# Router weights by a DRAM broadcast, and the values of four batches together with q and k, in a four-block transformer on one core

## The chip, the core and the metric

The kernel runs on one core of a Trainium2 chip. The metric is device time in microseconds for one execution, as the median of several runs. TensorE is the matmul engine, VectorE, ScalarE and GpSimd are the three engines for elementwise work, and SyncE issues most of the DMAs. Every engine works through its own queue in order.

## The reference

Input x has 32 batches of 128 tokens and 144 channels. Four blocks follow one another; each is steered by a condition vector per batch.

```python
x = _L0_cond_ref(x, ...)   # attention with normalised q, k; MLP
x = _L1_cond_ref(x, ...)   # rotation by expm of a skew matrix, per batch
x = _L2_cond_ref(x, ...)   # attention, MLP
x = _L3_cond_ref(x, ...)   # attention, mixture of experts
```

What matters here is the attention of L2 and L3, and the router and the experts of L3:

```python
h = _modulate(_ln(x), sh_msa, sc_msa)
qkv = (h @ w_qkv + b_qkv).reshape(B, N, 3, nh, hd).transpose(2, 0, 3, 1, 4)
q, k, v = (qkv[0], qkv[1], qkv[2])
attn = softmax(einsum('bhqd,bhkd->bhqk', q, k) * hd ** (-0.5))
...
xn = _modulate(_ln(x), sh_mlp, sc_mlp)
gate_logits = xf @ w_gate                      # 4 experts
topk_logits, topk_idx = top_k(gate_logits, 2)
gates = softmax(topk_logits)
cw = sum(one_hot(topk_idx, 4) * gates[..., None], axis=1)
hmid = gelu(einsum('tc,ech->eth', xf, w1) + b1)
eo = einsum('eth,ehc->etc', hmid, w2) + b2
moe = einsum('te,etc->tc', cw, eo)
```

## The kernel before

All of x stays in SBUF as `x_sb` (128 tokens by 32 batches by 144). The batches go in groups of four (`G`). The 144 channels are split into a main part of 128 rows and a remainder of 16. `ln_T` (L678) normalises, transposes and modulates a group: `hM` holds the main parts; the remainders of the four batches come into one tile `hG` of 128 rows (32 for each batch), which a round trip through DRAM (`hD`) spreads into `hR`, where each of four groups of 32 rows holds the remainders of all four batches. So a product with 144 channels is a main matmul of 128 rows and a remainder matmul of 32 rows on one of four row tiles of the array. `both` (L715) issues the mains of several products and then the remainders, or the other way round, and yields between the two.

PSUM has eight banks: one is `ps_o`, the other seven rotate in order of allocation (`bank`, L82).

The order of the work is written out by hand. The main loop (L1435) runs over ticks, one batch of attention in each. Within a tick it calls `scores` (L880) for half the heads, `weigh` (L939, probabilities by values), `scores` for the other half, and the closing steps (`largest_T`, `largest`, `project_out`, `project_sum`), and between these named gaps ("a", "e", "t", "stats", "b0", "b", "den", "pre1", "c", "y1", "y2", "y3", "z", "d") that `fill` (L1422) fills with whatever `put(tick, gap, f, ...)` has put there. `put2` puts the two halves of a function that yields once in two gaps. The block L0 is layer 0, L2 is layer 1 and L3 is layer 2 in these names; L1, the rotation, is done between them. A group of layer n starts at tick `t0`; its MLP or experts run at `t0 + 7` and later, beside the attention of later groups and layers.

Around the change:

- `qk_chunks` (L752), in gap "c" of `t0 - 2`, makes q and k of a group: three banks of 128x512, three mains, three remainders on row tiles 0 to 2. ScalarE copies them to `qT` and `kT`, and SyncE moves nine rows of each of four heads within SBUF.
- `values` (L851) makes the values of two batches at a time, as tokens by channels, in layers 1 and 2 at `t0` and `t0 + 1`: two banks, two mains (`ps_v`, L720), two remainders on two row tiles, and then four VectorE copies (L863, L864) straight from PSUM into `vaug`.
- `gate_logits` (L1096), at `t0 + 7` in gaps "den" and "c": four mains and four remainders (L1102), the latter with `hR`. `expert_ranks` and `expert_weights` (L1110, L1133) make `cw` at `t0 + 8`, with the last product at L1139.
- `moe1` makes the hidden layer of a pair of experts in three parts; the two experts share one tile of it, `hid[:, SHARED]`, 64 rows each. `shared_by_gate` (L1166) multiplies that tile by the router's weights: GpSimd spreads `cw` to `cwx` (L1171) in "stats", four transposes (L1175) bring it to a bank in "y1", and VectorE multiplies (L1176). This is done for both pairs of a group, at `t0 + 8` and `t0 + 10`.
- `moe2_parts` (L1182) follows in "y2" and "y3": eight records of `ps_f` with the unshared tiles (L1187), then the shared tile (L1192), then two VectorE sums into `acc` (L1196, L1198). In layer 2 the first pair of a group's values stands between the two halves, in "y2".
- `moe_out` (L1200), at `t0 + 12` in gap "b", which is `t0 + 8` of the next group: GpSimd multiplies `acc` by a gate and adds it to x (L1205, L1206), and SyncE writes the group out (L1207).

Matrix products in fp32 stand in the profile as two records each, transposes as one.

Of the kernel before, what the change touches and what calls it, by code (L numbers as in the profile page):

```python
# [8 lines left out]
F32 = mybir.dt.float32  # L9
# [3 lines left out]
ALU = mybir.AluOpType  # L13
# [56 lines left out]
def tile_kernel(ctx: ExitStack, tc: tile.TileContext, a: dict, out: bass.AP):  # L70
# [181 lines left out]
        nms.append(t)  # L252

    take_nm = ring([128, 128], "nm", 2, fill_nm)
    take_kT = ring([128, 4, G * T], "kT", 2, lambda t: None)
    take_qk = ring([128, 32, SLOT], "qkn", 2, fill_qk)
    take_v = ring([128, 2 * NH, 32], "vaug", 2, fill_v)
# [86 lines left out]
    def prep_qr():  # L344


        ala = pq.tile([128, D], F32, name="ala")
        tri = cst[:, K_TRI : K_TRI + D]
        for j in range(D):
            n = C - j  # L350
            cols = slice(j, C + j + 1)
            ps = bank([128, C + 1], f"ps_qr{j}")
            nc.tensor.matmul(
                ps, ident[:, j : j + 1].to_broadcast([128, 128]), at[:, cols], start=True, stop=True
            )
# [38 lines left out]
        nc.vector.tensor_scalar(sgn, sgn, 2.0, -1.0, ALU.mult, ALU.add)  # L394
        nc.vector.tensor_tensor(v[:, :D], v[:, :D], dg, ALU.add)
        yield
        yield
        ps = bank([D, D], "ps_yr")
        nc.tensor.matmul(ps, ident[D:, D:], at[D:, :D], start=True, stop=True)
        y = pq.tile([D, D], F32, name="y")  # L400
        nc.scalar.copy(y, ps)
        yield
        ps = bank([128, C + 1], "ps_uT")
        for h in range(2):
            rows = slice(h * D, (h + 1) * D)
# [12 lines left out]
        nc.gpsimd.memset(uR, 0.0)  # L418
        yield
        yield  # L420
        ps = bank([128, 2, D], "ps_u")
        nc.tensor.transpose(ps[:, 0, :], uT[:D, :CM], idd)
        nc.tensor.transpose(ps[:, 1, :], ur, idd)
        nc.vector.tensor_copy(uM, ps[:, 0, :])
        for i in range(G):
            nc.vector.tensor_copy(uR[rows4(i), i, :], ps[rows4(i), 1, :])

    def prep_expm():

# [322 lines left out]
    def qk_chunks(g):  # L752
# [7 lines left out]
        yield from both(  # L760
            [(ps, p.wqk[:, c], hM) for ps, c in zip(pss, cols)],
            [(ps, p.wqkR[rows4(m), cols[m]], hR[rows4(m)]) for m, ps in enumerate(pss)],
            False,
        )
# [11 lines left out]
        for j in range(4):  # L776
            r = 32 * j + 1
            nc.sync.dma_start(
                kT[r : r + HD, 3, :], qT[r + PITCH : r + PITCH + HD, 1, :]
            )  # L780

    def qk_masked(g):
        kT, k = gr[g].pop("k")
# [311 lines left out]

    def gate_logits(g):  # L1096
        gr[g]["lg"] = lg = small.tile([128, G, E], F32, tag="lg", name=f"lg_{g[1]}", bufs=2)
        hM, hR = gr[g]["hM_m"], gr[g]["hR_m"]
        ps = bank([128, T], f"ps_g_{g[1]}")
        for w, h in ((L3.wgate, hM), (L3.wgateR, hR)):  # L1100
            for i in range(G):
                nc.tensor.matmul(ps[rows4(i)], w, h[:, i, :], start=h is hM, stop=h is hR)  # L1102
        lgT = late.tile([128, T], F32, tag="lgT", name=f"lgT_{g[1]}")
        nc.scalar.copy(lgT, ps)
        yield
# [4 lines left out]
    def expert_ranks(g):  # L1110
# [2 lines left out]
        lg = gr[g]["lg"]  # L1113
        sh = [128, G, E]
        sh4 = [128, G, E, E]
        cw = small.tile(sh, F32, tag="cw", name=f"cw_{g[1]}", bufs=2)
        rank = small.tile(sh, F32, tag="rank", name=f"rank_{g[1]}", bufs=2)
        one = small.tile([128, G, 1], F32, tag="one", name=f"one_{g[1]}", bufs=2)
        gt = small.tile(sh4, F32, tag="gt", name=f"gt_{g[1]}", bufs=2)
# [46 lines left out]
    def shared_by_gate(g, pair):  # L1166


        cwx = late.tile([128, G, 2, 64], F32, tag="cwx", name=f"cwx_{g[1]}_{pair}", bufs=1)
        cw = gr[g]["cw"][:, :, 2 * pair : 2 * pair + 2]  # L1170
        nc.gpsimd.tensor_copy(cwx, cw.unsqueeze(3).to_broadcast([128, G, 2, 64]))  # L1171
        yield
        ps = bank([128, G, T], f"ps_cw_{g[1]}_{pair}")
        for i in range(G):
            nc.tensor.transpose(ps[:, i, :], cwx[:, i, :, :].rearrange("p e c -> p (e c)"), ident)  # L1175
        nc.vector.tensor_tensor(hid[:, SHARED], hid[:, SHARED], ps, ALU.mult)  # L1176

    def moe2(g, e, i):
        for _ in moe2_parts(g, e, i):
# [142 lines left out]
    for layer in range(3):  # L1322
        ahead = 5 if layer == 0 else 6
        for n in range(NG):
# [34 lines left out]
            if layer == 0:  # L1359
                for i in (0, 2):  # L1360
                    put2(t0 + i // 2, "stats", "b", values, g, i, 2, True)
            elif layer == 1:
                put2(t0, "stats", "b", values, g, 0, 2, True)
                put2(t0 + 1, "stats", "b", values, g, 2, 2, True)
            else:
                put2(t0, "y2", "y2", values, g, 0, 2, True)
                put2(t0 + 1, "den", "pre1", values, g, 2, 2)
            if layer:
                put2(t0 - 2, "c", "c", qk_chunks, g)
                if g == (1, 0):  # L1370
# [15 lines left out]
                for i in range(G):  # L1386
                    put(t0 + (10, 10, 11, 11)[i], "bdbc"[i], mlp2, g, i)
            else:
                put2(t0 + 7, "den", "c", gate_logits, g)
                put(t0 + 8, "e", expert_ranks, g)  # L1390
                put(t0 + 8, "stats", expert_weights, g)
                for i in range(G):
                    put(t0 + 8 + i // 2, "cdab"[i], moe_bias, g, i, n == NG - 1)
                for pair in range(2):
# [4 lines left out]
                    else:  # L1399
                        put2(at_, "den", "pre1", moe1, g, pair, 1, False)  # L1400
                    put2(at_ + 1, "stats", "b0", moe1, g, pair, 2, True)
                    put2(at_, "stats", "y1", shared_by_gate, g, pair)
                    put2(at_, "y2", "y3", moe2_parts, g, 2 * pair, 0)
                    put(at_ + 1, "b", moe2, g, 2 * pair, 1)
                    put(at_ + 1, "c", moe2, g, 2 * pair, 2)
# [10 lines left out]
    put(-4, "z", without_means)  # L1416

    put(first[1] - 2, "a", lambda: [zeros(t) for t in nms])
    put(first[1] + B - 10, "c", load_L3)
    put(first[1] + B + 7, "d", lambda: load_pair(1, mlps[:, :PAIR_COLS]))  # L1420

    def fill(tick, gap):  # L1422
# [12 lines left out]
    for tick in range(-6, first[2] + B + 14):  # L1435
# [13 lines left out]
        fill(tick, "stats")  # L1449
        if s2 is not None:  # L1450
            weigh(s2)
        fill(tick, "b0")
        fill(tick, "b")
        fill(tick, "den")
# [209 lines left out]
```

## Time and profile before

| | |
|---|---|
| median of 3 runs | 1283.43 us (1283.4 to 1290.53) |
| profiled execution | 1298.18 us, span 1296.5 us |
| mean granted TensorE clock | 0.988 |
| `ps_cw` L1175, 64 transposes | 10.4 us busy |
| `ps_v` L720, layers 0 and 1: 128 main and 128 remainder records | 23.6 and 14.8 us busy |
| `ps_v` L720, layer 2: 64 main and 64 remainder records | 11.5 and 8.2 us busy |
| `ps_qk` L720, remainders, 96 records | 18.2 us busy |
| VectorE L1176, 16 products of 128x512 | 10.9 us busy, 682 ns each |
| VectorE L863 and L864, 128 copies of 128x72 | 28.5 us busy |
| TensorE waiting for `hR_m` at L1102 | 4.4 us in 2 places, the longest 4.0 |

Busy times are unions of the records of one kind, so 64 overlapping transposes of 285 ns each come to 10.4 us. In a timeline, what an operation costs TensorE is the distance from its start to the start of what follows. Bracketed times are the engine's idle time before a record, with what released it. SyncE's rows show the issue of a DMA, not its transfer.

### The profile page before, as it was taken

The page shows a single profiled execution, that of the slowest core. Times are in us where ns is not written, and L with a number is a line of the kernel's source. Part 1 is how long each engine was busy: PE and PEld are TensorE (multiplying, and loading weights), DVE is VectorE, ACT ScalarE, POOL GpSimd, SP SyncE. Part 2 cuts the span into 40 slices and gives each one's busy share as a digit, 9 for nine tenths or more (in the row PEclk, how much of TensorE's full clock was granted, in tenths as well). Part 3 has the DMA queues.
Part 4 walks back from the last instruction along what each step waited for, and adds up shares of the span by engine and source line. Part 5 has one row for each costly group of instructions (what it writes and reads, how often), then busy time and mean ns, then how long its engine had stood idle before and what let it go on. Part 6 is the DMA issues. An engine that isn't in the chain of part 4 may idle for free.

```text
span 1296.5 us, 35389 instructions
## 1 busy us (share of the span) xinstructions
PE 1243.1 (96%) x13980; PEld 909.2 (70%) x13980; DVE 809.9 (62%) x2543; ACT 779.3 (60%) x1724; POOL 668.4 (52%) x1642
## 2 busy tenths in 40 slices
PE   6889888999998999999999999999999999999998
PEld 5668667778766677677777766667676767677656
DVE  5488888876775467676667666446454646455343
ACT  2457677688685656667666666555555555555431
POOL 5467767756663545454545454636363636251610
PEclk9989999999998999999999999999999999999999
DMA  8200011010013111111121111210101010100000
GB/s 223 65 14 23 16 36 37 2 37 11 30 36 112 62 47 35 46 55 37 47 85 55 55 38 54 76 54 10 55 10 54 11 54 11 54 20 17 20 26 10
DMA packets 50328, 56.44 MB, mean 44 GB/s; under 512 B 4688, under 2 KB 35792, under 8 KB 49904
## 3 DMA queue, kind: packets, MB, share of 16 engines
q1 hardware_dynamic: 49504, 53.70, 13.7%
q8 instruction: 113, 1.85, 0.6%
q10 hardware_dynamic: 656, 0.44, 0.2%
q14 instruction: 55, 0.45, 0.1%
HBM read 39.94 MB, written 13.00 MB: 41 GB/s over the span
## 4 chain that ended last, share of the span: by engine, by line
PE 67%; DVE 3%; DMA 2%; ACT 1%; SPq 1%; issue 0%; POOL 0%; DVEq 0%
PE ps_h L720 19%; PE ps_f L1187 10%; PE ps_s L917 6%; PE ps_w L917 6%; PE ps_o L948 5%; PE ps_qk L720 5%; PE ps_f L1042 4%; PE ps_pj L1012 3%; PE ps_v L720 2%; PE ps_f L1192 1%; DVE nm L929 1%; PE ps_o L869 1%; DMA hD_m<-hG_m 1%; DMA hR_m<-hD_m 1%; PE ps_hT_m L689 1%; PE ps_cw L1175 1%
## 5 line engine op out<-in xcount | busy, mean ns | idle before, releaser
L929 DVE TENSOR_REDUCE nm<-ps_s 128x4 f32<-128x512 f32 x384 | 246.4, 683 | 101.8 <-PE ps_w L917 80.5
L933 ACT ACTIVATE pr<-ps_w 128x512 f32<-128x512 f32 x384 | 208.5, 595 | 150.0 <-PE ps_w L917 141.2
L917 PE MATMUL ps_s<-kT,qT 32*128 32x256 f32 (+2 forms) x1536 | 238.3, 413 | 0.9 <-ACT kT L849 0.9
L917 PE MATMUL ps_w<-q,kT 32*128 32x128 f32 x3072 | 233.7, 287 | 0.0
L917 PEld LDWEIGHTS ps_w<-q,kT 32*128 32x128 f32 x3072 | 197.7, 190 | 11.2 <-issue 6.3
L1036 ACT ACTIVATE hid<-ps_h 128x512 f32<-128x512 f32 (+1 forms) x224 | 119.9, 590 | 101.8 <-PE ps_h L720 101.4
L917 PEld LDWEIGHTS ps_s<-kT,qT 32*128 32x128 f32 x1536 | 138.3, 188 | 30.2 <-issue 10.0
L720 PE MATMUL ps_h<-hM_m,mlps 128*128 128x512 f32 x304 | 144.1, 607 | 0.0
L1196 DVE SCALAR_TENSOR_TENSOR acc<-ps_f,cw,acc 128x144 f32<-128x144 f32 x128 | 46.7, 366 | 148.0 <-PE ps_f L1187 72.9
L998 POOL TENSOR_TENSOR x_sb<-x_sb,res_a 128x144 f32<-128x144 f32 x96 | 46.9, 489 | 158.8 <-DVE res_a L1001 158.0
L948 PE MATMUL ps_o<-pr,vaug 128*32 128x128 f32 x3072 | 105.8, 279 | 0.0
L948 PEld LDWEIGHTS ps_o<-pr,vaug 128*32 128x32 f32 x3072 | 79.4, 111 | 33.7 <-PE ps_w L917 17.4
L720 PEld LDWEIGHTS ps_h<-hM_m,mlps 128*128 128x128 f32 x304 | 53.3, 189 | 67.6 <-issue 66.5
L1042 PE MATMUL ps_f<-mlps,hid 128*128 128x144 f32 x640 | 94.7, 296 | 0.0
L1042 PEld LDWEIGHTS ps_f<-mlps,hid 128*128 128x128 f32 x640 | 83.4, 192 | 8.9 <-issue 4.6
L933 ACT ACT_TABLE_LOAD x57 | 73.1, 1283 | 10.0 <-PE ps_w L917 9.1
L792 POOL TENSOR_SCALAR kT<-kT,cst 128x512 f32<-128x512 f32 x30 | 46.8, 1561 | 58.5 <-ACT kT L774 57.0
L1033 ACT ACT_TABLE_LOAD x58 | 74.4, 1283 | 1.0
L660 POOL TENSOR_SCALAR rs_m_a<-mv_m_a 128x2 f32<-128x2 f32 x81 | 15.5, 191 | 114.3 <-DVE mv_m_a L658 86.5
L1187 PEld LDWEIGHTS ps_f<-pair,hid 128*128 128x128 f32 x512 | 66.9, 190 | 8.4 <-issue 7.7
L1187 PEld LDWEIGHTS ps_f<-mlps,hid 128*128 128x128 f32 x512 | 66.7, 190 | 8.1 <-issue 7.4
L1187 PE MATMUL ps_f<-mlps,hid 128*128 128x144 f32 x512 | 71.3, 288 | 0.0
(337 smaller groups left out, 2747.0 us busy)
## 6 DMA issues: line engine op xcount, KB each, us to landing
gates<-gates SPq DMA_DIRECT2D x48, 288.0 KB
hD_m<-hG_m SPq DMA_DIRECT2D x24, 256.0 KB
hR_m<-hD_m SPq DMA_DIRECT2D x24, 256.0 KB
hD_a<-hG_a SPq DMA_DIRECT2D x16, 256.0 KB
hR_a<-hD_a SPq DMA_DIRECT2D x16, 256.0 KB
x_sb<-in_x SPq DMA_DIRECT2D x8, 288.0 KB
out_x<-x_sb SPq DMA_DIRECT2D x7, 288.0 KB
mlps<-in_L_mlp SPq DMA_DIRECT2D x2, 1000.0 KB
```

Of the source, the lines that this page charges most:

```text
L720: nc.tensor.matmul(ps, x, y, start=k == 0, stop=k == 1)
L792: eng.tensor_scalar(o, k, m, None, ALU.mult)
L917: nc.tensor.matmul(o, x, y, start=True, stop=True)
L929: nc.vector.tensor_reduce(to, view, AX.X, ALU.max, negate=True)
L933: nc.scalar.activation(pr[:, 4 * e : 4 * e + 4, :].rearrange("p s q -> p (s q)"), view, AF.Exp, scale=SCALE,)
L948: nc.tensor.matmul(po[rows4(j), t, :], v[:, 4 * j + 2 * t + r, :], prs[j // 2][:, 4 * (j % 2) + 2 * r + t, :], start=r == 0, stop=r == 1,)
L998: nc.gpsimd.tensor_tensor(x_sb[:, b, :], x_sb[:, b, :], t, ALU.add)
L1033: nc.scalar.activation(t, half, AF.Gelu_apprx_tanh)
L1036: nc.scalar.activation(hid[:n, i], ps[:n], AF.Gelu_apprx_tanh)
L1042: nc.tensor.matmul(ps, hid[:, at0, i, :], w2[:, m, :], start=m == 0, stop=m == NFC - 1)
L1187: nc.tensor.matmul(ps[:, 0, :], hid[:, at0 + m, i, :], w2[:, at0 + m, :], start=m == 0, stop=m == 3)
L1196: nc.vector.scalar_tensor_tensor(acc, ps[:, 0, :], w, acc, ALU.mult, ALU.add)
```

## The change

1. `shared_by_gate` loses the spreading, the transposes and the bank. A new `gate_rows`, at `t0 + 8` in "den", transposes the weights of all four experts and four batches at once (they now lie in a zeroed 128x128 tile `cwz`), ScalarE copies 16 rows out, and SyncE writes them to DRAM and reads each expert's row back into 64 partitions, for the first pair at once and for the second at `t0 + 9`.
2. `gate_logits` takes its remainders from `hG`, with weights that are zero outside one batch's rows, and its first half moves to a new gap "o", right behind `weigh`.
3. In layers 1 and 2 `qk_chunks` makes the values of all four batches too, two batches in a bank, their remainders all on row tile 3. `values_raw` (VectorE, "z" of the same tick) copies the two banks to SBUF, and `values_spread` (VectorE, "b" of `t0` and `t0 + 1`) spreads them into `vaug`.
4. The rotation's `uR` is made by one VectorE product with a mask instead of a GpSimd zeroing and four copies, two yields later, and L3's weights are loaded one tick later.

```diff
@@ qk_chunks
+        pvs = [bank([128, 2, C], f"ps_v_{g[0]}_{g[1]}_{n}") for n in range(2)]
+        pv, r3 = [pvs[i // 2][:, i % 2, :] for i in range(G)], rows4(3)
+        for ps, c in zip(pss, cols):
+            nc.tensor.matmul(ps, p.wqk[:, c], hM, start=True, stop=False)
+        for i, ps in enumerate(pv):
+            nc.tensor.matmul(ps, hM[:, i, :], p.wv, start=i % 2 == 0, stop=False)
+        yield
+        for m, ps in enumerate(pss):
+            nc.tensor.matmul(
+                ps, p.wqkR[rows4(m), cols[m]], hR[rows4(m)], start=False, stop=True
+            )
+        for i, ps in enumerate(pv):
+            nc.tensor.matmul(ps, hR[r3, i, :], p.wvR[r3], start=False, stop=i % 2 == 1)
+        gr[g]["v"] = pvs
...
+    def values_raw(g):
+        for n, ps in enumerate(gr[g].pop("v")):
+            raw = work.tile(QS, F32, tag="qkraw", name=f"vraw_{g[0]}_{g[1]}_{n}")
+            nc.vector.tensor_copy(
+                raw.rearrange("p s d -> p (s d)"), ps.rearrange("p i c -> p (i c)")
+            )
+            gr[g]["v", n] = raw
+
+    def values_spread(g, n):
+        pair, src = take_v(), gr[g].pop(("v", n)).rearrange("p (q r) d -> p q r d", r=2)
...
+        for r in range(2):
+            nc.vector.tensor_copy(v[:, :, 48 * r : 48 * r + HD], src[:, :, r, :])
@@ gate_logits
-        for w, h in ((L3.wgate, hM), (L3.wgateR, hR)):
-            for i in range(G):
-                nc.tensor.matmul(ps[rows4(i)], w, h[:, i, :], start=h is hM, stop=h is hR)
+        for i in range(G):
+            nc.tensor.matmul(ps[rows4(i)], L3.wgate, hM[:, i, :], start=True, stop=False)
+        for i in range(G):
+            nc.tensor.matmul(
+                ps[rows4(i)], L3.wgateR[:, 32 * i : 32 * i + 32], hG, start=False, stop=True
+            )
@@ expert_ranks
-        cw = small.tile(sh, F32, tag="cw", name=f"cw_{g[1]}", bufs=2)
+        gr[g]["cwz"] = take_cw()
+        cw = gr[g]["cwz"][:, : E * G].rearrange("p (e i) -> p i e", i=G)
@@ shared_by_gate
-        cwx = late.tile([128, G, 2, 64], F32, tag="cwx", name=f"cwx_{g[1]}_{pair}", bufs=1)
-        cw = gr[g]["cw"][:, :, 2 * pair : 2 * pair + 2]
-        nc.gpsimd.tensor_copy(cwx, cw.unsqueeze(3).to_broadcast([128, G, 2, 64]))
-        yield
-        ps = bank([128, G, T], f"ps_cw_{g[1]}_{pair}")
-        for i in range(G):
-            nc.tensor.transpose(ps[:, i, :], cwx[:, i, :, :].rearrange("p e c -> p (e c)"), ident)
-        nc.vector.tensor_tensor(hid[:, SHARED], hid[:, SHARED], ps, ALU.mult)
+        ws = gr[g]["cwb"].rearrange("p (i t) -> p i t", i=G)
+        nc.vector.tensor_tensor(hid[:, SHARED], hid[:, SHARED], ws, ALU.mult)
+
+    def gate_rows(g):
+        ps = bank([128, 128], f"ps_cw_{g[1]}")
+        nc.tensor.transpose(ps, gr[g]["cwz"], ident)
+        rows = late.tile([128, T], F32, tag="lgT", name=f"cwT_{g[1]}")[: E * G]
+        nc.scalar.copy(rows, ps[: E * G])
+        gr[g]["cwD"] = dram.tile([E * G * T], F32, name=f"cwD_{g[1]}")
+        nc.sync.dma_start(gr[g]["cwD"].rearrange("(r t) -> r t", t=T), rows)
+        gate_rows_of(g, 0)
+
+    def gate_rows_of(g, pair):
+        ws = gr[g]["cwb"] = late.tile([128, G * T], F32, tag="cwb", name=f"cwb_{g[1]}_{pair}")
+        for e in range(2):
+            at0 = (2 * pair + e) * G * T
+            nc.sync.dma_start(
+                ws[64 * e : 64 * e + 64], gr[g]["cwD"][at0 : at0 + G * T].partition_broadcast(64)
+            )
@@ the plan
-                put2(t0, "stats", "b", values, g, 0, 2, True)
-                put2(t0 + 1, "stats", "b", values, g, 2, 2, True)
-            else:
-                put2(t0, "y2", "y2", values, g, 0, 2, True)
-                put2(t0 + 1, "den", "pre1", values, g, 2, 2)
+                put(t0 - 2, "z", values_raw, g)
+                for n_ in range(2):
+                    put(t0 + n_, "b", values_spread, g, n_)
...
-                put2(t0 + 7, "den", "c", gate_logits, g)
+                put2(t0 + 7, "o", "c", gate_logits, g)
+                put(t0 + 8, "den", gate_rows, g)
+                put(t0 + 9, "den", gate_rows_of, g, 1)
...
-                    put2(at_, "stats", "y1", shared_by_gate, g, pair)
+                    put(at_, "y1", shared_by_gate, g, pair)
```

More of the change, by code (lines that the diff above doesn't have):

```diff
@@ L254, in tile_kernel @@
     take_nm = ring([128, 128], "nm", 2, fill_nm)
+    take_cw = ring([128, 128], "cwz", 2, zeros)
     take_kT = ring([128, 4, G * T], "kT", 2, lambda t: None)
@@ L417, in prep_qr @@
         )
-        nc.gpsimd.memset(uR, 0.0)
-        yield
-        yield
+        for _ in range(4):
+            yield
         ps = bank([128, 2, D], "ps_u")
@@ L424, in prep_qr @@
         nc.vector.tensor_copy(uM, ps[:, 0, :])
-        for i in range(G):
-            nc.vector.tensor_copy(uR[rows4(i), i, :], ps[rows4(i), 1, :])
+        nc.vector.tensor_tensor(
+            uR, ps[:, 1, :].unsqueeze(1).to_broadcast([128, G, D]),
+            cst[:, K_M4 : K_M4 + G].unsqueeze(2).to_broadcast([128, G, D]), ALU.mult,
+        )
     def prep_expm():
@@ L759, in qk_chunks @@
         cols = [slice(128 * m, 128 * m + 128) for m in range(3)]
[L760 to L764, printed above, removed]
+        pvs = [bank([128, 2, C], f"ps_v_{g[0]}_{g[1]}_{n}") for n in range(2)]
[4 more added lines that the diff above has]
+            nc.tensor.matmul(ps, hM[:, i, :], p.wv, start=i % 2 == 0, stop=False)
+        yield
+        for m, ps in enumerate(pss):
[5 more added lines that the diff above has]
+        gr[g]["v"] = pvs
         nc.scalar.copy(qT[:, 0, :], pss[0])
@@ L780, in qk_chunks @@
             )
+    def values_raw(g):
[7 more added lines that the diff above has]
+        pair, src = take_v(), gr[g].pop(("v", n)).rearrange("p (q r) d -> p q r d", r=2)
+        for i in range(2):
+            st[g[0] * B + g[1] * G + 2 * n + i]["v"] = pair[:, i * NH : (i + 1) * NH, :]
+        v = pair.rearrange("p (q r) s -> p q (r s)", r=2)
+        for r in range(2):
+            nc.vector.tensor_copy(v[:, :, 48 * r : 48 * r + HD], src[:, :, r, :])
     def qk_masked(g):
@@ L1097, in gate_logits @@
         gr[g]["lg"] = lg = small.tile([128, G, E], F32, tag="lg", name=f"lg_{g[1]}", bufs=2)
-        hM, hR = gr[g]["hM_m"], gr[g]["hR_m"]
+        hM, hG = gr[g]["hM_m"], gr[g]["hG_m"]
         ps = bank([128, T], f"ps_g_{g[1]}")
-        for w, h in ((L3.wgate, hM), (L3.wgateR, hR)):
-            for i in range(G):
-                nc.tensor.matmul(ps[rows4(i)], w, h[:, i, :], start=h is hM, stop=h is hR)
+        for i in range(G):
[4 more added lines that the diff above has]
+            )
         lgT = late.tile([128, T], F32, tag="lgT", name=f"lgT_{g[1]}")
@@ L1166, in shared_by_gate @@
     def shared_by_gate(g, pair):
-        cwx = late.tile([128, G, 2, 64], F32, tag="cwx", name=f"cwx_{g[1]}_{pair}", bufs=1)
-        cw = gr[g]["cw"][:, :, 2 * pair : 2 * pair + 2]
-        nc.gpsimd.tensor_copy(cwx, cw.unsqueeze(3).to_broadcast([128, G, 2, 64]))
-        yield
-        ps = bank([128, G, T], f"ps_cw_{g[1]}_{pair}")
-        for i in range(G):
-            nc.tensor.transpose(ps[:, i, :], cwx[:, i, :, :].rearrange("p e c -> p (e c)"), ident)
-        nc.vector.tensor_tensor(hid[:, SHARED], hid[:, SHARED], ps, ALU.mult)
+        ws = gr[g]["cwb"].rearrange("p (i t) -> p i t", i=G)
[14 more added lines that the diff above has]
+                ws[64 * e : 64 * e + 64], gr[g]["cwD"][at0 : at0 + G * T].partition_broadcast(64)
+            )
     def moe2(g, e, i):
@@ L1361, in tile_kernel @@
                     put2(t0 + i // 2, "stats", "b", values, g, i, 2, True)
-            elif layer == 1:
-                put2(t0, "stats", "b", values, g, 0, 2, True)
-                put2(t0 + 1, "stats", "b", values, g, 2, 2, True)
-            else:
-                put2(t0, "y2", "y2", values, g, 0, 2, True)
-                put2(t0 + 1, "den", "pre1", values, g, 2, 2)
+            else:
+                put(t0 - 2, "z", values_raw, g)
+                for n_ in range(2):
+                    put(t0 + n_, "b", values_spread, g, n_)
             if layer:
@@ L1418, in tile_kernel @@
     put(first[1] - 2, "a", lambda: [zeros(t) for t in nms])
-    put(first[1] + B - 10, "c", load_L3)
+    put(first[1] + B - 9, "c", load_L3)
     put(first[1] + B + 7, "d", lambda: load_pair(1, mlps[:, :PAIR_COLS]))
@@ L1451, in tile_kernel @@
             weigh(s2)
+        fill(tick, "o")
         fill(tick, "b0")
@@ L1619 @@
     main_and_rest("L3_wgate", w, np.zeros(32, w.dtype), 1)
+    rest = np.zeros((32, G, G, 32), w.dtype)
+    for i in range(G):
+        rest[:CR, i, i, :] = w[CM:]
+    arrays["L3_wgateR"] = rest.reshape(128, 128)
     for name, (wn, bn) in _MOD.items():
```

## The prediction

> **What bounds the kernel now.** I read the page first (busy time by engine, then the chain of work that ended last), then the timeline of every engine through one tick of the third block, then SyncE's queue, then the granted clock by stretches.
>
> ```profile
> PE 1243.1 (96%) x13980; PEld 909.2 (70%) x13980; DVE 809.9 (62%) x2543; ACT 779.3 (60%) x1724; POOL 668.4 (52%) x1642
> PE 67%; DVE 3%; DMA 2%; ACT 1%; SPq 1%; issue 0%; POOL 0%; DVEq 0%
> ```
>
> TensorE is the bound: 96% busy, and two thirds of the chain. So a matmul that goes is worth its pitch (start of one to start of the next, not its 0.27 us of latency), and a wait that comes to stand in TensorE's queue costs all of its length. Only 53 us of the span are not busy, so later slack cannot pay it back.
>
> The tick that matters is the one in which a group's first expert pair meets the router's weights. From the second group's (TensorE, then VectorE, GpSimd, SyncE; columns are start, duration, engine, line, shape):
>
> ```profile
> 892.48 0.28 PE L917 MATMUL ps_w<-q,kT 32*128 32x128 f32 x2
> ...
> 893.46 0.66 PE L1175 MATMUL ps_cw<-cst,cwx 128*128 128x128 f32 x4
> 893.96 1.15 PE L1187 MATMUL ps_f<-pair,hid 128*128 128x144 f32 x8
> 895.03 0.51 PE L720 MATMUL ps_v<-rotU,hR_a 32*128 32x144 f32 x4
> 895.48 0.76 PE L720 MATMUL ps_v<-rotU,hM_a 128*128 128x144 f32 x4
> 896.07 0.41 PE L1192 MATMUL ps_f<-pair,hid 128*128 128x144 f32 x2
> ...
> 893.55 1.29 DVE L929 TENSOR_REDUCE nm<-ps_s 128x4 f32<-128x512 f32 x2 [2.37 <-PE ps_w L917]
> 894.76 0.68 DVE L1176 TENSOR_TENSOR hid<-hid,ps_cw 128x512 f32<-128x512 f32 x1
> ...
> 890.98 1.46 POOL L1206 TENSOR_TENSOR x_sb<-x_sb,acc 128x576 f32<-128x576 f32 x1
> ...
> 892.47 0.39 SPq L1207 DMA_DIRECT2D out_x<-x_sb  x1
> ```
>
> The reader should see three things. L1192 needs VectorE's product L1176, which ends at 895.44; the value matmuls between L1187 and L1192 cover that wait. The product itself waits for the two reduces, not for the transposes. And SyncE stands at out_x until GpSimd's L1206 is through, 892.47: whatever is queued behind out_x is issued after that.
>
> The last view is the clock by stretches (columns: from and to, length, TensorE's busy time and instructions, granted clock, DMA share, GB/s):
>
> ```profile
> 810.37:813.78 3.41, 0.71 (x16) 1.00 0.23 77
> 813.78:817.19 3.41, 3.41 (x32) 0.50 0.00 0
> ```
>
> TensorE stood from 809.12 to 813.07, 3.95 us, at the gate's remainder matmuls (L1102) for hR_m. The stretch after it ran at half clock: scores took 1.75 us (813.43 to 815.18; elsewhere 1.11, 1067.86 to 1068.97), L1042's ten records 2.30 (elsewhere 1.33). That is 1.6 us on top of the wait.
>
> **The change, part by part.** All sums are against this execution: 1298.18 us, of which the span is 1296.5. It lies 14.75 us (1.1%) above the median 1283.43; I carry the difference over unchanged.
>
> Transposes. Sixteen times four L1175 transposes go, 0.50 us each time (893.46 to 893.96): -8.0. Eight single ones come, at the pitch of 0.11 us (L869 at 896.32, L689 at 896.42): +0.9. Together -7.1 us. The copy cwx on GpSimd (0.61 us) goes too, but GpSimd then still waits for acc; nothing gained.
>
> Values. A group's four batches now cost, in the third block, 0.45 + 0.59 for the first pair (above) and 0.59 + about 0.2 for the second, 1.85 us; in the second block 1.75 (0.60 twice, remainders 0.2 beside scores and 0.35 alone). Afterwards the eight main records take 8 x 0.15 = 1.2 us. The eight remainder records, all on the fourth row tile, are queued behind those of q and k, which take 1.07 us on three tiles (1056.12 to 1057.19). One tile does such a record in 0.124 us (sixteen L917 records on two tiles, 1210.75 to 1211.74), 0.14 for 144 columns, so they need 1.1 us: free if tiles run side by side, +1.1 if not. Scores and weights of different tiles do overlap (L917 above), so I take 0.1. That makes 1.3 a group, -0.55 eight times and -0.45 eight times: -8 us; the other end is +8.
>
> VectorE of the values. Eight copies of 0.22 us become two of 128x288 out of PSUM (0.41 to 0.45, from L874's 128x256 and L832's 128x288) and four of 128x144 (0.22 to 0.30). The four lie where VectorE idles 2.37 us, so they cost nothing; without that idle, 1.2 us a group. The two stand at the end of the q,k tick, behind acc and q, and the next tick's second score waits for the first one's bank, its weights for the second's: in the fourth such tick L1192 starts at 1058.69, VectorE's q ends 1.6 us later (1060.28), two copies more make 2.4, and TensorE begins its weights at 1.65 (1060.34). So +0.8 us in six groups of the third block: +5 (0 to 10).
>
> Gate logits read hG instead of hR, so L1102 waits for no DMA: -3.95 and -1.6 for the clock, -5.6 us.
>
> The router's weights now go ScalarE copy, DRAM, broadcast, VectorE. In the six groups with an out_x of the group before (second to seventh), the DRAM write stands behind it on SyncE. SyncE's next issue came 0.44 after an out_x (1150.02, 1150.46): write at 892.91. Its landing: modD, 16 KB on quiet queues, released the next issue 1.43 us later (50.38, 51.81), hD_m, 256 KB, 2.23 us later (1062.55, 1064.78). So the first broadcast goes at 894.3 to 895.15, the second 0.4 after. A broadcast: hR_m, 256 KB, woke TensorE 2.57 us after its issue (810.50, 813.07); two of 128 KB, 2.57 to 3.0. VectorE starts its product at 896.9 to 898.15 and ends at 897.6 to 898.8. TensorE, rid of the transposes and the values, has done L1187 at 893.46 + 0.11 + 1.08 = 894.65. The stall is 2.95 to 4.2 us; I take 3.6, because the write's packets follow out_x's own 288 KB. Six times: 21.6. In the last group out_x is issued at 1258.42; by the same steps the product ends at 1263.5 to 1264.8, TensorE is ready at about 1258.5, and 0.84 of that wait is there now: +4.8. In the first group no out_x stands ahead, and only the reduces hold the product: 0.9. Sum +27.3 (22 to 32). Behind the waiting product stand acc, q and the residual, and TensorE waits for them all anyway. For the second pair the weights are fetched a tick ahead; no stall.
>
> The clock. A stall of 3.6 us lies so in a 3.41 us stretch that it leaves at most 1.6 us of work in one of them; the row above had 0.71 and cost 1.6. Seven stalls: +11.4 (0 to 16).
>
> The rest: uR in one operation, two memsets at the start, L3's weights a tick later (loaded at 665 now, first used at 728): nothing.
>
> Sum: -7.1 - 8 + 5 - 5.6 + 27.3 + 11.4 = +23 us, 1306.
>
> The Trainium skill speaks of this clock in "TensorE: Matmul & The Clock Gate", What's actually happening: the clock halves after at least one idle window of about 3.4 us, free-running. Read as wholly idle, a 3.6 us stall would fill one in about 6% of cases, and the sum would be +12 instead of +23. The row here, a stretch with 0.71 us of work in it, was followed by half clock all the same, so the trace decides for +23.
>
> **The rivals.** (1) The stall is real but the clock stays: +12, 1295, 0.9% slower. For it: several stretches with about 2 us of work before 400 us kept full clock. Against it: the stretch shown. (2) The weights arrive in time. If SyncE issued the write when ScalarE has the rows (transpose at 888.85, copy by 889.5), then 1.43 + 0.4 + 2.57 give 893.9, before the reduces end at 894.84; then only 0.9 us of stall is left in each group: -7.1 - 8 + 5 - 5.6 + 6.5 = -9, 1274, and with the raw copies hidden as well -14, 1269. It turns on out_x: the write must be issued some 2.5 us before out_x is now. Against it: the program puts the write behind out_x, and that waits for GpSimd's sum. This is the case on the other side. (3) The fourth tile's remainders run after the other three's: +16 more, 1322. Against it is the overlap of tiles in L917's rows.
>
> **How the numbers follow.** Forecast 0.57, rival (1) 0.18, (2) 0.15, (3) 0.10. About 1%, 13 us, is what a measurement of this kernel tells from no change. Slower by more: the forecast, (3), and nearly half of (1), 0.75. Within: the rest of (1) and two thirds of (2), less a little of each for the other side, 0.17. Faster: 0.08. The range leaves out (2) and a little above: from 1284, which is the forecast with low stalls and no clock loss, to 1322.
>
> **What would show it.** In the profile after: TensorE idle before the second matmul group of an expert pair's first part (the L1192 of now), released by VectorE's product, 3 to 4 us in six groups; VectorE idle ahead of that product, released by the broadcast; SyncE's write issued within half a microsecond of out_x; seven half-clock stretches after 820 us; no wait at the gate near 810; the q,k remainders at 1.1 to 1.3 us with the values' beside them. I am wrong if the broadcast lands before the reduces are done, or if TensorE has other work to do while it waits.

## The result and the profile after

| | before | after |
|---|---|---|
| median | 1286.45 us (1283.4 to 1290.53, 4 runs) | 1324.93 us (1321.99 to 1329.57, 4 runs) |
| ratio, 95% interval | | 1.0267 (1.023 to 1.0305) |
| profiled execution | 1298.18 us | 1326.36 us, span 1324.6 us |
| mean granted TensorE clock | 0.988 | 0.973 |
| third block, from the first `hD_m` of it to the end of the span | 488.2 us | 523.1 us |

The change is slower, as forecast, and by more: 2.7%, where 1.8% (23 of 1283 us) was said. The time lies 3 us above the range's upper end and 19 us above the forecast. The first two lines are from the page of after, busy time and then the chain that ended last.

```profile
PE 1237.5 (93%) x13924; PEld 916.4 (69%) x13924; DVE 811.6 (61%) x2508; ACT 781.0 (59%) x1732; POOL 662.4 (50%) x1627
...
PE 62%; DVE 6%; DMA 3%; ACT 2%; issue 1%; POOL 0%; SPq 0%; DVEq 0%; POOLq 0%
```

TensorE has 5.6 us less work than before (1243.1) in a span that is 28.1 us longer, and the chain now has 9% of VectorE and DMA where it had 5%. Which wait is new stands in the list of waits (engine and line, what it waited for; us in total, times, longest):

```profile
PE ps_f L1234 <- DVE hid L1201: 37.9, 9, 6.9
DVE hid L1201 <- DMA cwb<-cwD: 33.6, 7, 7.5
```

L1234 is the matmul with the shared hidden tile (L1192 before), L1201 VectorE's product with the router's weights (L1176 before). TensorE waits for VectorE, and VectorE for the broadcast. The timeline of the second group shows how that comes about (start, duration, engine, line; in brackets the idle time before and its releaser):

```profile
877.33 0.26 ACT L1207 COPY cwT<-ps_cw 16x128 f32<-16x128 f32 x1 [1.46 <-PE ps_cw L1205]
...
879.23 1.49 POOL L1248 TENSOR_TENSOR x_sb<-x_sb,acc 128x576 f32<-128x576 f32 x1
...
880.75 0.39 SPq L1249 DMA_DIRECT2D out_x<-x_sb  x1
...
881.24 0.44 SPq L1209 DMA_DIRECT2D cwD<-cwT  x1
...
881.75 1.25 PE L1229 MATMUL ps_f<-pair,hid 128*128 128x144 f32 x8
881.84 1.29 DVE L956 TENSOR_REDUCE nm<-ps_s 128x4 f32<-128x512 f32 x2 [2.38 <-PE ps_w L944]
...
883.72 5.34 SPq L1216 DMA_DIRECT2D cwb<-cwD  x4
...
887.26 0.69 DVE L1201 TENSOR_TENSOR hid<-hid,cwb 128x512 f32<-128x512 f32 x1 [4.12 <-DMA cwb<-cwD]
888.00 0.50 PEld L1234 LDWEIGHTS ps_f<-pair,hid 128*128 128x128 f32 x2 [5.22 <-DVE hid L1201]
888.00 0.84 PE L1234 MATMUL ps_f<-pair,hid 128*128 128x144 f32 x2 [5.00 <-DVE hid L1201]
```

ScalarE has the rows at 877.59 (L1207), but SyncE stands at out_x until GpSimd's L1248 is through, and issues the write at 881.24. The first broadcast goes 2.48 us after the write, the product starts 3.54 after that. The stalls of the first pairs at L1234 are 0.92, 5.00, 4.81, 4.64, 5.43, 4.80, 4.66 and 6.88 us, group by group: 37.1 (the list has one of a second pair besides). The clock around this stall (from and to, length, busy time of PE, PEld, DVE, ACT, POOL, then granted clock, DMA share, GB/s):

```profile
881.64:885.06 3.42, 1.36 (x14) 1.03 (x8) 1.29 (x2) 3.27 (x5) 3.17 (x8) 1.00 0.31 93
885.06:888.47 3.41, 0.47 (x2) 0.47 (x3) 0.69 (x1) 0.00 (x0) 1.81 (x5) 0.50 0.25 75
888.47:891.89 3.42, 3.42 (x29) 3.13 (x32) 1.31 (x4) 0.81 (x2) 1.02 (x3) 0.50 0.22 77
891.89:895.30 3.41, 3.41 (x53) 1.88 (x48) 2.06 (x6) 2.18 (x4) 2.99 (x8) 1.00 0.02 5
```

The stretch in which the stall began had 1.36 us of work; the two after it ran at half clock. One of them is full of work. There are seven such half-clock spells after 820 us, one for each long stall: twelve stretches, 41 us in all.

A second measure serves the experiments. Over all eleven profiled executions the ninth `hD_m` (the first of the second block) is issued anywhere from 500.8 to 517.0 us, with 17 to 31 us of half clock ahead of 420 us in every kernel, before among them; from there to the first `hD_m` of the third block it is 290.2 to 291.4 us in all of them. So what differs from run to run lies ahead of these two parts, and the third block, from its first `hD_m` to the end, compares two kernels without that difference. The second block, measured so, took 291.3 us before and 290.2 after. Within the third block, "half ticks" run from the first record of `scores` to that of the next half of the heads; eight make a group, and where nothing is late they repeat in the middle groups within 0.1 us (H7 of before and of e4 alone varies by 0.2 to 0.3). These are of one group each (us; H2 holds the first expert pair, H6 q and k and the second pair):

```
            H1     H2     H3    H4    H5     H6    H7    H8    sum
before     10.30   5.69   8.24  6.72  10.30  8.64  7.81  6.64  64.34
after      10.41  10.55   7.67  7.13  10.30  9.23  8.03  6.64  69.96
e1         10.41   5.34   7.46  7.16  10.30  9.23  8.03  6.64  64.57
e2         10.31   5.21   7.46  7.14  10.30  9.74  7.89  6.64  64.69
e4         10.30   5.21   7.46  7.15  10.31  9.74  8.03  6.64  64.84
e5         10.30   5.21   7.46  6.70  10.30  9.74  7.89  6.65  64.25
e6         10.41   5.21   7.47  6.91  10.30  9.22  8.03  6.64  64.19
e7         10.30   5.68   8.24  6.73  10.30  8.64  7.66  6.64  64.19
e8         10.41   9.28   7.47  7.24  10.30  9.22  8.04  6.64  68.60
e9         10.42   5.36   7.47  6.69  10.30  9.22  8.04  6.64  64.14
```

### The profile page after: what moved, and what is told of

It is laid out like the page before. It is cut to its first block, busy times and chain, and to the rows that moved or that the text cites. A ratio compares the mean times of both kernels' runs of the same rounds, so it can differ in the third digit from the quotient of the medians.

```text
span 1324.6 us, 35285 instructions
## 1 busy us (share of the span) xinstructions
PE 1237.5 (93%) x13924; PEld 916.4 (69%) x13924; DVE 811.6 (61%) x2508; ACT 781.0 (59%) x1732; POOL 662.4 (50%) x1627
## 4 chain that ended last, share of the span: by engine, by line
PE 62%; DVE 6%; DMA 3%; ACT 2%; issue 1%; POOL 0%; SPq 0%; DVEq 0%; POOLq 0%
PE ps_h L722 18%; PE ps_f L1229 8%; PE ps_s L944 6%; PE ps_w L944 5%; PE ps_o L975 5%; PE ps_f L1069 4%; PE ps_qk L765 3%; PE ps_pj L1039 3%; DVE nm L956 2%; DMA cwb<-cwD 2%; PE ps_f L1234 1%; DMA cwD<-cwT 1%; PE ps_v L767 1%; PE ps_o L896 1%; PE ps_v L774 1%
## 5 line engine op out<-in xcount | busy, mean ns | idle before, releaser
L1238 DVE SCALAR_TENSOR_TENSOR acc<-ps_f,cwz,acc 128x144 f32<-128x144 f32 x128 | 46.8, 366 | 176.7 <-PE ps_f L1234 102.2
L1069 PE MATMUL ps_f<-mlps,hid 128*128 128x144 f32 x640 | 93.7, 294 | 0.0
L702 ACT ACTIVATE hM_m<-ps_hT_m,modM 128x128 f32<-128x128 f32 x96 | 44.8, 467 | 70.2 <-PE ps_hT_m L691 69.3
L960 ACT ACT_TABLE_LOAD x57 | 73.1, 1283 | 9.5 <-PE ps_w L944 8.5
L1060 ACT ACT_TABLE_LOAD x58 | 74.4, 1283 | 1.0
```

Of the source, the lines that this page charges most:

```text
L960: nc.scalar.activation(pr[:, 4 * e : 4 * e + 4, :].rearrange("p s q -> p (s q)"), view, AF.Exp, scale=SCALE,)
L1060: nc.scalar.activation(t, half, AF.Gelu_apprx_tanh)
L1069: nc.tensor.matmul(ps, hid[:, at0, i, :], w2[:, m, :], start=m == 0, stop=m == NFC - 1)
L1238: nc.vector.scalar_tensor_tensor(acc, ps[:, 0, :], w, acc, ALU.mult, ALU.add)
```

## The experiments

All of them together; ratios are to the kernel before on the same chip, whose medians there were 1290.86 (22 runs, beside e1 to e4), 1289.81 (22, beside e5 to e8) and 1291.65 us (13, beside e9).

| | median us | ratio (95%) | third block us |
|---|---|---|---|
| e1 out_x behind the weights | 1284.82 | 0.9962 (0.9935 to 0.9989) | 487.5 |
| e2 transposes kept | 1280.68 | 0.9917 (0.9886 to 0.9949) | 482.6 |
| e3 24 matmuls in the stall | 1318.14 | 1.0207 (1.0155 to 1.0258) | 521.8 |
| e4 values alone | 1289.65 | 0.9989 (0.9955 to 1.0023) | 491.3 |
| e5 = e2, copies earlier | 1281.53 | 0.9926 (0.9902 to 0.995) | 479.8 |
| e6 = e5, second pair by DRAM | 1278.42 | 0.9903 (0.9868 to 0.9938) | 479.5 |
| e7 gate logits alone | 1285.28 | 0.9953 (0.9925 to 0.998) | 481.1 |
| e8 16 matmuls in the stall | 1315.39 | 1.0168 (1.0117 to 1.0218) | 515.7 |
| e9 rows earlier | 1280.08 | 0.9909 (0.9876 to 0.9943) | 478.7 |

**e1: is it the place behind out_x, or the way through DRAM?**

```diff
-                    put(t0 + 12, "b", moe_out, g)
+                    put(t0 + 12, "pre1", moe_out, g)
```

> The changed kernel with one step moved: the store of the group before (out_x) stands behind the write and the two broadcasts of the router's weights on SyncE; the order on every other engine is as it was. Theory: the weights are late because their write stands behind out_x, which waits for GpSimd. Then SyncE issues the write as soon as ScalarE has the rows (877.59 in the second group, where it was 881.24), the write lands as fast as in the first group (1.36 us), the product waits for the two reduces alone, and the stall at the second part of the expert pair falls from 4.6 to 6.9 us to about 0.9 in the second to eighth group: about 30 us less, and 10 to 12 less of half clock. 1276 to 1288 us. Rival: the way through DRAM is too long wherever it begins (3.5 us from the issue of a broadcast to the product, 2.2 to 2.5 for the write): then 3 us of stall are left and the time is 1305 to 1318.

Measured: 1284.82 us, 40 below the changed kernel. The timeline of its second group:

```profile
866.97 0.32 SPq L1209 DMA_DIRECT2D cwD<-cwT  x1
...
868.37 1.39 SPq L1216 DMA_DIRECT2D cwb<-cwD  x2
...
870.10 0.40 SPq L1249 DMA_DIRECT2D out_x<-x_sb  x1
...
871.20 1.29 DVE L956 TENSOR_REDUCE nm<-ps_s 128x4 f32<-128x512 f32 x2 [2.38 <-PE ps_w L944]
...
872.57 0.69 DVE L1201 TENSOR_TENSOR hid<-hid,cwb 128x512 f32<-128x512 f32 x1
...
873.32 0.39 PE L1234 MATMUL ps_f<-pair,hid 128*128 128x144 f32 x1 [0.96 <-DVE hid L1201]
```

The write lands in 1.40 us, the product starts right behind the reduces with no bracket of its own, and the stall is 0.96. The stalls sum to 9.7 us instead of 37.1. With one step moved on one queue (VectorE, ScalarE and GpSimd have the same instructions in the same order in both traces), 35.6 us of the third block go: 27.4 of stall, and 8.2 more, for which e8 below shows the clock. The rival is out for most groups. It holds in part: in the fourth and fifth group the write landed in 2.21 and 2.33 us, with stalls of about 1.5, and in the last group, which has little other work for TensorE, 2.74 us of stall are left, with half clock after it.

Line numbers differ a little from kernel to kernel.

**e2: everything but the DRAM weights.** `shared_by_gate` as before, `gate_rows`, `gate_rows_of` and the zeroed tile taken out:

```diff
-        ws = gr[g]["cwb"].rearrange("p (i t) -> p i t", i=G)
-        nc.vector.tensor_tensor(hid[:, SHARED], hid[:, SHARED], ws, ALU.mult)
+        nc.gpsimd.tensor_copy(cwx, cw.unsqueeze(3).to_broadcast([128, G, 2, 64]))
+        yield
+        ps = bank([128, G, T], f"ps_cw_{g[1]}_{pair}")
+        for i in range(G):
+            nc.tensor.transpose(ps[:, i, :], cwx[:, i, :, :].rearrange("p e c -> p (e c)"), ident)
+        nc.vector.tensor_tensor(hid[:, SHARED], hid[:, SHARED], ps, ALU.mult)
```

> The changed kernel with the router's weights spread as before (cwx on GpSimd, four transposes a pair, product out of PSUM); the values with q and k and the gate logits from hG stay. Theory: the values give 8 us less on TensorE and 5 more at the raw copies, the gate logits 5.6 less, all against the kernel before: about 1278 us (1274 to 1283), with no stall at the second part of an expert pair and no half clock after 820. Rival: the remainders of the values on the fourth row tile run after the other three and the raw copies hold the scores: 1288 to 1300.

Measured: 1280.68 us and a ratio of 0.9917, no half clock between 820 us and the last few. The rest of the change is a gain. e1 is 4.9 us of the third block slower than this: even with its queue free, the DRAM way as placed here costs more than the transposes that it saves. Nearly all of it is the last group: from the last `hD_m` to the end e1 takes 61.7 us and e2 57.4; in all that stands ahead, e1 costs 0.6 us more.

**e3: is the clock lost to the stall?**

```diff
+        if e == 0 and i == 0:
+            for _ in range(24):
+                nc.tensor.matmul(ps[:, 1, :], hid[:, 0, i, :], w2[:, 0, :], start=True, stop=True)
```

> The changed kernel with 24 matmuls of 144 columns (0.15 us each, 3.6 us) put in front of the one that stalls, into the bank that it overwrites; they wait for nothing that is late. Theory: the stalls of the second to eighth group (4.6 to 6.9 us) take the work in, TensorE is busy in the stretch and keeps its clock. The first group, whose stall is 0.9, pays 2.7. What is left of the half clock then goes: 1324.9 less 10 to 12 plus 2.7, 1314 to 1318 us, although 29 us of work were added. Rival: the half clock after the stalls has another cause: 1325 to 1330 with half-clock stretches as before. Second rival: TensorE is not idle there: 1350.

Measured: 1318.14 us, and no half clock after 800 us in its profile but at the very end. But each of these matmuls is two records and takes 0.245 us, so 5.9 us of work were added instead of 3.6: the stall was overfilled, H2 became 10.04 (e1: 5.34), and the size of the clock's share can't be read from it. So it was made again:

**e8: work that is shorter than the stall.** The same with `range(16)`, and `and g[1]` in the condition (not in the first group).

> The changed kernel with 16 matmuls of 144 columns (at 0.245 us each as e3 showed, 3.9 us) in front of the stalling one, in the second to eighth group alone: less than the stall (4.6 to 6.9 us), so that the stall keeps its length and only the clock can change. Theory: TensorE is busy in the stretch, the half clock after the stalls goes (1.4 to 2.5 us a group by the half ticks of the changed kernel), 11 to 13 us less: 1312 to 1314. Rival: the clock falls for another cause, or the loss at half clock is small: 1322 to 1325.

Its second group (timeline), and the granted clock from there on (columns as above):

```profile
878.13 1.25 PE L1229 MATMUL ps_f<-pair,hid 128*128 128x144 f32 x8
879.21 4.08 PE L1235 MATMUL ps_f<-pair,hid 128*128 128x144 f32 x32
884.51 0.51 PE L1237 MATMUL ps_f<-pair,hid 128*128 128x144 f32 x2 [1.21 <-DVE hid L1201]
```

```profile
881.00:884.41 3.41, 2.30 (x19) 2.08 (x17) 0.65 (x1) 0.31 (x1) 2.20 (x5) 1.00 0.24 77
884.41:887.82 3.41, 3.31 (x39) 2.60 (x39) 1.78 (x6) 1.15 (x3) 1.27 (x4) 1.00 0.26 82
```

L1237 is the matmul that stalls, and no earlier (1.21 us of wait and 3.92 of added work, where 5.00 of wait were), and the clock stays at 1.00 in six of the seven groups; in the last, 3.27 us of wait are left, and 6.83 us of half clock follow. With 27 us of useless work added the kernel is 9.5 us faster than the changed one by the medians and 7.5 by the third block, a little under the 11 to 13 expected. So the half clock comes from the stall, and costs about 8 us.

**e4: the values alone**, on the kernel before: the edits to `qk_chunks`, `values_raw`, `values_spread` and their places in the plan, as the change has them, with the small fourth part of the change.

> The kernel before with the values of four batches together with q and k in the second and third block, and nothing else of the change but the small things of the preparation. Theory: -8 us on TensorE, +5 at the raw copies: about 3 less than before, 1280 to 1286 us, with the gate's wait and its half clock still there. Rival: the remainders on the fourth row tile are serial (+16): 1295 to 1302.

Measured: a ratio of 0.9989; neither side of 1 is excluded. By the parts: the second block is 1.0 us shorter, the third 3.1 longer. About half of the 3.1 is the gate: its wait stays in this kernel, two stretches of half clock follow it (801.1 to 808.0 us) where before had one, and the first group takes 62.5 us instead of 61.0. TensorE in the q,k half tick:

```profile
1046.12 1.14 PE L766 MATMUL ps_v<-rotU,hM_a 128*128 128x144 f32 x8
1047.20 0.70 PE L769 MATMUL ps_qk<-hR_a,rotU 32*128 32x512 f32 x3
1047.22 0.75 PE L773 MATMUL ps_v<-rotU,hR_a 32*128 32x144 f32 x4
1047.73 0.60 PE L769 MATMUL ps_qk<-hR_a,rotU 32*128 32x512 f32 x3
1047.81 0.65 PE L773 MATMUL ps_v<-rotU,hR_a 32*128 32x144 f32 x4
1048.39 0.66 PE L1201 MATMUL ps_cw<-cst,cwx 128*128 128x128 f32 x4
```

The remainders of the values (L773) run beside those of q and k (L769): 1.19 us together (1047.20 to 1048.39), where q and k alone took 1.07. The serial rival is out. What the values gave up is less than forecast: H2 falls by 0.48 and H3 by 0.78, but H4 grows by 0.43. In H4 VectorE is late:

```profile
1088.91 0.59 PE L943 MATMUL ps_s<-kT,qT 32*128 32x384 f32 x2
...
1089.02 0.37 DVE L1222 SCALAR_TENSOR_TENSOR acc<-ps_f,cw,acc 128x144 f32<-128x144 f32 x1 [3.91 <-PE ps_f L1218]
...
1089.64 0.39 DVE L806 COPY vaug<-vraw 128x144 f32<-128x144 f32 x2
...
1091.68 1.28 DVE L955 TENSOR_REDUCE nm<-ps_s 128x4 f32<-128x512 f32 x2
...
1093.01 0.33 PE L895 MATMUL ps_o<-cst,nm 128*128 128x128 f32 x1 [0.28 <-DVE nm L955]
```

VectorE works without a break from 1089.02, the reduces start 2.77 us after the scores (2.34 before), and TensorE waits for them at L895. The spreading copies (L806) stand behind the expert sums (L1222), which VectorE has waited 3.9 us for.

**e5: the copies into that wait.** On e2:

```diff
-                    put(t0 + n_, "b", values_spread, g, n_)
+                    put(t0 + n_, "o", values_spread, g, n_)
```

> The kernel of e2 with the four spreading copies of the values ahead of the expert sums (acc) in VectorE's order instead of behind them. Theory: the values give less than forecast because two of the half ticks of a group in the third block that they left are now set by VectorE: in e4 the scores come 0.8 us earlier and the half tick after them is 0.42 longer, its reduces late behind acc, acc and the copies. Ahead of acc the copies lie in VectorE's wait for TensorE (3.9 us there), the half tick falls from 7.14 back to about 6.7 us, seven times: 3 us less than e2, 1277 to 1279. Rival: the half tick is set by acc, and the copies' place changes nothing: 1280 to 1281.

Measured: H4 falls from 7.14 to 6.70 and the third block from 482.6 to 479.8, 2.8 us, as expected. The medians (1281.53, of 1274.34 to 1286.43) don't tell it from e2; their intervals are wider than the step.

**e6: DRAM where there is time.** On e5, `gate_rows` without its first pair, and in `shared_by_gate`:

```diff
+        if pair:
+            yield
+            ws = gr[g]["cwb"].rearrange("p (i t) -> p i t", i=G)
+            nc.vector.tensor_tensor(hid[:, SHARED], hid[:, SHARED], ws, ALU.mult)
+            return
```

> The kernel of e5 with the router's weights of the second expert pair alone by way of DRAM and a broadcast, a tick ahead of their use; the first pair keeps the transposes. Theory: the way through DRAM costs only where it is waited for; a tick ahead it takes the four transposes and their product from PSUM off the half tick (9.23 us in the changed kernel, 9.74 in e2) and costs one transpose (0.1 us): 0.4 us less eight times, 3 less than e5, 1274 to 1276. Rival: the broadcasts, behind out_x on SyncE, hold up what follows there, or the product still waits: same as e5 or slower.

Measured: H6 falls by 0.52 as expected, H1 pays 0.11 for the transpose, but H4 and H7 are 0.21 and 0.14 longer: the third block is the same as e5's within 0.3 us. A miss: the two longer half ticks were not foreseen. H4's 0.21 stands in one VectorE instruction, the product `oT`: at the same place it takes 0.65 us where e5's takes 0.43, and the reduces behind it start 0.22 us later. Why it takes longer is not shown, nor is the cause of H7's 0.14. The ratio of 0.9903, the lowest ratio of all, does not tell it from e5 either.

**e7: the gate logits alone**, on the kernel before (the edit to `gate_logits`, its gap and the packed weights).

> The kernel before with the gate logits from hG alone. Theory: the wait at the gate's remainders (3.95 us) and the half clock after it (1.6) go, in the third block alone: 5.6 us less than before, ratio 0.9955, and the first group of the third block takes 55.5 us instead of 61. If the values are then worth the 3 us that were forecast for them, e2 is 3 us below this kernel; if they cost, e2 is not below it. Rival: TensorE waits for the same transfer at its next use: no gain, ratio 1.000.

Measured: a ratio of 0.9953, and the first group of the third block (its `hD_m` to the next) at 55.9 us instead of 61.0. e2 is 1.5 us above it in the third block and 1.2 below in the second: by these parts the values, as the change places their copies, are worth nothing. The medians put e2 4.6 us below e7, with intervals of the ratios that overlap.

**e9: the weights sooner, out_x left alone.** On the changed kernel, with e5's move and:

```diff
-                put(t0 + 8, "den", gate_rows, g)
...
+                put(t0 + 8, "b0", gate_rows, g)
```

behind the first part of `moe1` in that gap, ahead of eight matmuls of the experts.

> The changed kernel with two steps moved: the transpose and copy of the router's rows stand ahead of the last eight expert matmuls of the tick instead of behind them, so that the write goes to SyncE about 2 us sooner and ahead of out_x without out_x being moved, and the spreading copies lie as in e5. Theory: what kept e1 from gaining was the length of the way through DRAM, which starts late enough to be waited for in the fourth, fifth and last group (stalls of 1.5 to 2.7 us, the last with half clock); 2 us sooner every product waits for its reduces alone, the stalls of the first pair sum to 7 us or less (e1: 9.7), no half clock is left but at the end, and with the copies' 2.7 us the time is 5 to 9 less than e1: 1276 to 1280. Rival: what kept e1 back lies elsewhere in the tick: 1281 to 1284, with e1's stalls.

Measured: 1280.08 us, a ratio of 0.9909; the stalls of the first pairs sum to 6.5 us (e1: 9.7), the write lands in 1.36 to 1.42 us in all eight groups, and there is no half clock. The list of waits, with one of a second pair, has left of the two rows of the changed kernel:

```profile
PE ps_f L1234 <- DVE hid L1201: 7.3, 8, 1.1
```

There is no row of VectorE waiting for cwb. The third block of e9, 478.7 us, is the shortest of all, 44.4 us below the changed kernel's and 8.8 below e1's, of which the copies' move is some 2.8 (e5). The last group, from its `hD_m` on, takes 56.7 us. So e1 was held back by the way through DRAM starting late. e5, e6 and e9 are faster than both kernels, by 0.7 to 1% of the one before; which of the three is the fastest, the runs don't tell.

## Why the prediction was right, and where its sizes were off

The side and the mechanism held. The write goes 0.49 us after out_x (0.44 said), VectorE waits for the broadcast, TensorE for VectorE, seven half-clock spells follow, the wait at the gate is gone. Both conditions named for being wrong failed to come. That the count of seven held is partly luck: one stretch for each stall was said, and there were two for most. Rival (1), a stall without half clock, fell with the profile and with e8. Rival (3), serial remainders, fell with e4. Rival (2) named the right hinge, out_x: in e1 the weights come in time, and the slowdown is gone.

The sizes, in the third block, as differences of neighbours (so they add up to the 34.9 us between before and after; the forecasts add up to 26.6, and with 3.6 off for the second block to the 23 of the sum):

| step | forecast us | measured us | from |
|---|---|---|---|
| gate logits | -5.6 | -7.1 | e7 less before |
| values and raw copies | -4.4 + 5 | +1.5 | e2 less e7 |
| weights by DRAM, if in time | -7.1 + 6.5 | +4.9 | e1 less e2 |
| stall by out_x | 27.3 - 6.5 | +27.4 | after less e1, idle at L1234 |
| clock | +11.4 | +8.2 | after less e1, the rest |

Three steps failed in size. The clock's term came out nearer, but not as reckoned: 1.6 us for each of seven stretches was said; the 8.2 us are the difference between twelve stretches and the two of e1, 0.8 us each.

The stall was forecast at 3.6 us (2.95 to 4.2) and came to 4.6 to 5.4, and 6.9 in the last group, where 0.84 + 4.8 was said. Two terms were short. The write: 1.43 to 2.23 us from issue to the next issue was taken from transfers that had the queue to themselves; behind out_x it was 2.16 to 2.98. The packets of the trace show why: in the second group out_x's 288 KB move from 881.67 to 882.72, the write's 8 KB from 882.56 to 882.76, 1.32 us after its issue; alone (e1) its first packet moves 0.82 us after the issue. The broadcasts: 2.57 to 3.0 us became 3.5 to 3.7 from the first issue to the product, 1.3 us to the first packet, 1.76 for 256 KB (885.02 to 886.78) and 0.5 to the product.

The weights in time were forecast to gain 0.6 us over the transposes, and cost 4.9. The step "If SyncE issued the write when ScalarE has the rows" took 1.43 + 0.4 + 2.57 = 4.4 us for the way; it is 1.4 + 3.5 to 3.8 (seventh and eighth group of e1), and the last group, where 4.3 of the 4.9 us stand, has too little work to hide it. Issued 2 us sooner (e9) it gains 1.1 on e5, near the forecast.

The values were to give 8 us on TensorE and take 5 on VectorE. They took less than said, 1.10 us in H6 (their matmuls, 1.3 said) and 0.2 in H7 (the raw copies, 0.8 said), and gave much less: 0.83 (0.48 + 0.78 - 0.43) of 1.85 us a group in the third block; the second block, with all costs, got 1.1 us shorter instead of 3.6. The step that failed is "The four lie where VectorE idles 2.37 us, so they cost nothing". The idle time is there, but the copies stand behind an instruction that waits, and the half tick is then VectorE's. The first pair's matmuls had moreover covered the wait for VectorE's product: TensorE stands 3.5 us for it in e4 (L1218, eight times) and 1.2 before (L1192). The prediction says so in its reading of the tick, and its term for the values doesn't subtract it.

The rest of the 19 us is the base: the forecast stood on a median of three runs, 1283.43, and 22 further runs of the kernel before have a median of 1290.86, 7.4 more. 1290.86 + 34.9 - 1.1 = 1324.7. So the steps account for 11 of the 19 us, and the base for 7. One sum of the prediction is not as its words have it: low stalls and no clock loss take the forecast to 1306 - 5.3 - 11.4 = 1289, and the range's lower end of 1284 needs the raw copies at nothing too.

## What to carry to other kernels

An operand that moves from TensorE to a DMA joins a queue: price it from the issue that stands ahead of it, with that issue's wait and its bytes, not from a transfer that was alone. A slow way needs its whole length ahead of its use: issued 2 us sooner, the way through DRAM went from 4.9 us dearer than the transposes (e1 and e2) to 1.1 cheaper (e9 and e5). And idle time of an engine hides a step only if the step stands in its queue ahead of what the engine waits for.

## What the runs showed of the hardware

The clock. The eleven profiled executions were cut into the stretches of 3.41 us in which the clock changes, from 50 us on and without the last 8 us. 46 stretches at full clock were followed by half clock; they held 0 to 2.27 us of TensorE work. None kept the clock with 1.72 us or less, about half of its length, and none lost it with more than 2.27; between 1.75 and 2.27 both occur. The Trainium skill, in "TensorE: Matmul & The Clock Gate", What's actually happening, puts the half clock after at least one idle window of about 3.4 us; here the stretch need not be idle, and the measurement decides. A stall shorter than the stretch is enough, as the last group of e1 shows (the wait, then the two stretches):

```profile
1239.03 0.56 PE L1234 MATMUL ps_f<-pair,hid 128*128 128x144 f32 x2 [2.74 <-DVE hid L1201]
```

```profile
1235.94:1239.36 3.42, 0.68 (x5) 0.43 (x4) 1.29 (x3) 0.10 (x2) 0.07 (x1) 1.00 0.50 161
1239.36:1242.77 3.41, 3.41 (x10) 1.23 (x9) 2.92 (x9) 0.00 (x0) 0.00 (x0) 0.50 0.21 77
```

Code loading and small transfers. The write of 8 KB is 16 packets of 512 bytes. With the queue free it landed in 1.36 to 1.43 us, but in 2.21 and 2.33 in two groups of e1; behind out_x in 2.15 to 2.23, but in 2.37 to 2.98 in eight places. Taken over the 40 writes of after, e1, e3, e8 and e9, each of these ten slow ones has a packet of the instruction queues (8 or 16 KB, 0.4 to 1.3 us long) in flight between its issue and its landing: 16 KB from 995.98 to 997.24 around the write issued at 996.16 in e1, 8 KB from 1062.37 to 1062.88 after the one issued at 1061.32, whose last packet starts only at 1062.88. Of the thirty others three have one, and there it ended 0.32 us after the issue or began 1.16 and 1.39 after it, while the write's own packets moved from 0.8 to 1.0. That the loading is the cause is read from the times of the packets; it was not tried.
